# In-place product without a reset operand, carry kept as a running sum, first near factor on VectorE, in a chunked selective scan

## The chip, the cores and the metric

One Trainium2 chip, one of its cores. The metric is the device time of one execution in microseconds; the kernel before takes 9089.72 us, the median of 3 runs (9088.7 to 9092.31).

## The reference

Two layers on 4 images of 64x64 positions with 192 channels. Only the first layer's scan is touched. It runs over the 4096 positions in four directions k (rows, columns, and both reversed), with 384 channels d and 16 states n:

```python
delta = softplus(dts + delta_bias)
# one step per position, for every direction k, channel d, state n:
h = exp(delta * A[n]) * h + delta * B[n] * u
y = sum over n of h[n] * C[n]
```

`A[n]` is -n here, so the decay of state n over a stretch is the n-th power of one factor. The four y are added and normed over the channels, multiplied by a gate and projected.

## The kernel before, in words

The first layer (`FirstLayer`, L575) has three parts, `project`, `scans` (L759) and `finish`. The change lies in `scans` and in the constants that feed it.

**Rounds and states.** The sequence of each direction is cut into blocks of 30 positions. A *round* r is one block of all four directions and four images; there are NR = 137. A tile of a round has 128 rows and W = 1536 columns (4 images x 384 channels). Each half of 64 rows holds two directions: rows 0 to 59 are positions, and the last four (60 to 63) are for what is carried between blocks. A round goes through its 16 states one after the other, `state(s) = 16 - s % 16`, so that the loop at L1093 has 2192 *steps* s.

**Step s.** TensorE's `mix` (L1072) adds `b` times `x` into two accumulators `accs[0]` and `accs[1]` in PSUM, each 128 x 768. VectorE's `weigh` (L1081) then multiplies each in place by `fd`, the factor exp(SHIFT - sum of delta), so that a state's sum has been multiplied n times at the end (a Horner scheme over the powers). It is one `scalar_tensor_tensor` (L1088): accumulator times a column `hold_n`, times `fd`. At state 1 `end_y` (L959), a `tensor_tensor`, writes the product to SBUF instead.

**x.** `grown` (L1059) makes the next power of the input factor, six steps ahead (`AHEAD`): `x[s] = x[s-1] * f`. GpSimd does the 1024 *far* columns with `f` from SBUF, VectorE the 512 *near* columns with `f0` from PSUM (both L1070). The first power of a round is `dtu * g` (L1066); GpSimd does all of it, in three instructions of 512 columns, with near last. The `g` comes from ScalarE: `first_far` (L901, two parts) and `first_near` (L913).

**b.** `outer` (L1049, TensorE) and `cut_b` (L1057, VectorE), once per two steps, make the 64x64 weight blocks from B, C and the masks. Columns 60 to 63 of a block collect the sum over a block of positions, for even and odd states in different columns.

**Carry.** After every odd state ScalarE copies both accumulators (`keep_end`, L1025) before `weigh` changes them. DMAs cut the four last rows into `small` (`shrink`, L1013), GpSimd multiplies by the block's decay (`settle`, L1038), a DMA stores it in DRAM (`carry_out`, L1041), and one round later `carry_in` (L1020) brings two rows per half into rows 60 and 61 of `x`. `hold_n` is 0 in the carry rows at odd states and 1 elsewhere, so a carry row is emptied after each pair of states.

**Order.** The order on every engine, and that of SyncE's DMAs, is written out by hand (`manual_schedule`, L1091). A round's preparation is put at steps relative to its start (`steps`, L971). Those that matter: at -7 `sums_near` (TensorE, L910), at -6 `first_near` and `fall_near` (ScalarE, L913 and L917), at -6, -4 and -2 three extra `sums_d` on TensorE whose result nobody reads. Inside a step, VectorE does `weigh` for j = 0 and 1, then `grown`, then `cut_b` at even steps, then what is planned. All of the preparation uses one PSUM tile `m` of two banks at a time (`ps_p`, one buffer). In the following, a state pair is named by its steps within a round, 0 to 15; step -6 of the next round is step 10.

Of the kernel before, what the change touches and what calls it, by code (L numbers as in the profile page):

```python
# [10 lines left out]
F32 = mybir.dt.float32  # L11
AF = mybir.ActivationFunctionType
ALU = mybir.AluOpType

NB, HW, CH = 4, 64, 192
L = HW * HW
DI, NS, DR, KD = 384, 16, 12, 4
ND = DI // 128
CB, NC2 = 96, 2
LC = 512  # L20
# [9 lines left out]
RW = 30  # L30
PART = 4
NR = -(-L // RW)
HALF = 64
LP = NR * RW + 2
ND2 = 2 * DI
W = NB * DI
SHIFT = 2.5
# [534 lines left out]
            yield True  # L572


class FirstLayer(Stage):  # L575

    def __init__(self, tc, ctx, consts, w, dram, good):
        nc = tc.nc  # L580
        self.tc, self.w = tc, w
        self.ident, self.group, self.one = consts
        self.good = good
        self.uT, self.bc, self.xd, self.y_row, self.y_col, self.carry, self.zeros = dram
        wp = ctx.enter_context(tc.tile_pool(name="wf", bufs=1))

        def load(name, shape):
            t = wp.tile(shape, F32, name=f"{name}_f")
            nc.sync.dma_start(t, w[name])
            return t  # L590

        self.w_xd = load("w_xd", [128, ND, 64])
        self.w_bc = load("w_bc", [128, ND, KD * 2 * NS])
        self.w_dt = load("w_dtk", [128, DI])
        self.masks = load("masks", [128, 2, HALF])
        self.hold = load("hold", [128, 2])
        self.late = load("late", [128, NS // 2])
        self.gamma = load("gamma", [128, ND])
        self.beta = load("beta", [128, ND])
        self.ln_eps = wp.tile([128, 1], F32, name="ln_eps_f")  # L600
        nc.vector.memset(self.ln_eps, 1e-6)
        self.gn_eps = wp.tile([128, 1], F32, name="gn_eps_f")
        nc.vector.memset(self.gn_eps, GN_EPS)
        self.shift = {}
        for by in (1.0, -1.0, -NS):
            self.shift[by] = wp.tile([128, 1], F32, name=f"shift_{len(self.shift)}")
            nc.vector.memset(self.shift[by], by * SHIFT)
        self.minus = wp.tile([128, 128], F32, name="minus_f")
        nc.vector.tensor_scalar_mul(self.minus, self.ident, -1.0)
        self.far = wp.tile([128, 4 * W // 64], F32, name="far_f")  # L610
        a_col = load("a_col", [128, 1])
        nc.scalar.activation(a_col, a_col, AF.Exp)
        self.tri = load("steps", [128, 128])
        nc.vector.tensor_scalar_mul(self.tri, self.tri, a_col)
        self.dsum = wp.tile([128, DI], F32, name="dsum_f")
        with tc.tile_pool(name="d4", bufs=1) as pd:
            d4 = pd.tile([128, KD, DI], F32, name="d4")
            nc.sync.dma_start(d4, w["D_rows"].partition_broadcast(128))
            nc.vector.tensor_add(self.dsum, d4[:, 0, :], d4[:, 1, :])
            nc.vector.tensor_add(self.dsum, self.dsum, d4[:, 2, :])  # L620
            nc.vector.tensor_add(self.dsum, self.dsum, d4[:, 3, :])

            a_log = pd.tile([128, KD, ND, NS], F32, name="a_log")
            nc.sync.dma_start(a_log, w["A_log"])
            ref = pd.tile([128, KD], F32, name="a_ref")
            nc.sync.dma_start(ref, w["a_ref"].partition_broadcast(128))
            ln_n = pd.tile([128, NS], F32, name="ln_n")
            nc.sync.dma_start(ln_n, w["ln_n"].partition_broadcast(128))
            for k in range(KD):
                nc.vector.tensor_scalar(a_log[:, k], a_log[:, k], ref[:, k : k + 1], None, ALU.subtract)  # L630
            nc.vector.tensor_tensor(a_log, a_log, bc(bc(ln_n, 1, KD), 2, ND), ALU.subtract)
            nc.vector.tensor_mul(a_log, a_log, a_log)
            nc.vector.tensor_scalar(a_log, a_log, 1e-12, None, ALU.is_le)
            top = pd.tile([128, 1], F32, name="a_top")
            nc.vector.tensor_reduce(top, a_log.rearrange("p k d n -> p (k d n)"), mybir.AxisListType.X, ALU.min)
            nc.vector.tensor_tensor(self.good, self.good, top, ALU.min)

            z = pd.tile([128, W], F32, name="z")
            nc.vector.memset(z, 0.0)
            nc.sync.dma_start(self.zeros, z[:RW])  # L640
            near, end = NR // 2 * RW, LP - L
            for t in (*self.uT, self.y_row, self.y_col):
                nc.sync.dma_start(t[L:], z[:end].rearrange("p (b e) -> p b e", b=NB))
            for t in (self.xd, self.bc):
                nc.sync.dma_start(t[:, :, L:], z[: t.shape[0], : NB * end].rearrange("p (b l) -> p b l", b=NB))
            nc.sync.dma_start(self.y_col[near : near + RW], z[:RW].rearrange("p (b e) -> p b e", b=NB))
            for t in self.carry:
                nc.sync.dma_start(t, z[:, : 4 * W // 64])

    def run(self, srcs, dsts, gates):  # L650
        self.project(srcs, gates)
# [107 lines left out]
    def scans(self):  # L759
        nc, tc = self.tc.nc, self.tc  # L760
        with ExitStack() as ctx:
# [44 lines left out]
            class Round:  # L806
# [90 lines left out]

                def first_far(self, i):
                    if i == 1:
                        self.g = p1.tile([128, W], F32, name="g", tag="l")  # L900
                    nc.scalar.activation(self.g[:, wide(i)], self.m[:, 0, :], AF.Exp, bias=shift[-NS], scale=float(NS))  # L901

                def fall_far(self, i):
                    if i == 1:
# [5 lines left out]
                    nc.tensor.matmul(self.m[:, 0, :], tri, self.dt[:, wide(0)], start=True, stop=True)  # L910

                def first_near(self):
                    nc.scalar.activation(self.g[:, wide(0)], self.m[:, 0, :], AF.Exp, bias=shift[-NS], scale=float(NS))  # L913

                def fall_near(self):
                    self.f0 = ps_f.tile([128, LC], F32, name="f0")
# [74 lines left out]
                    r += [(at, "pe", s(self.sums_d, 0)) for at in (-6, -4, -2)]  # L991
                    return r

            w_dt, one, shift, zeros, hold, late = self.w_dt, self.one, self.shift, self.zeros, self.hold, self.late
            uT, bc_dram, xd_dram, y_row, y_col, carry = self.uT, self.bc, self.xd, self.y_row, self.y_col, self.carry
            MIDDLE = NR // 2
            AHEAD = 6
# [16 lines left out]

            def carry_in(s):
                n = state(s)
                v = carry[(n - 1) // 2].rearrange("(c p q r k) f -> p r q c (k f)", c=2, p=2, q=2, r=2)
                for r in range(2):
                    to = xs[s][r * HALF + 2 * RW : r * HALF + 2 * RW + 2].rearrange("q (c f) -> q c f", c=2)
                    nc.sync.dma_start(to, v[n % 2, r])  # L1020

            def keep_end(s, j):
                if j == 0:
# [14 lines left out]
                nc.gpsimd.tensor_tensor(back[s], back[s], small[s], ALU.mult)  # L1038

            def carry_out(s):  # L1040
                nc.sync.dma_start(carry[(state(s) - 1) // 2], back[s])  # L1041

            def outer(s):
                outs[s] = ps_o.tile([128, LC], F32, name="o")
# [14 lines left out]
            def grown(s, engine):  # L1059
                it = of(s)  # L1060
                if s not in xs:
                    xs[s] = p_x.tile([128, W], F32, name="x")
                if s % NS == 0:
                    if engine is nc.gpsimd:
                        for i in (1, 2, 0):
                            engine.tensor_tensor(xs[s][:, wide(i)], it.dtu[:, wide(i)], it.g[:, wide(i)], ALU.mult)  # L1066
                    return
                part = slice(0, LC) if engine is nc.vector else slice(LC, W)
                f = it.f0 if engine is nc.vector else it.f
                engine.tensor_tensor(xs[s][:, part], xs[s - 1][:, part], f, ALU.mult)  # L1070
# [10 lines left out]
            def weigh(s, j):  # L1081
                n = state(s)
                if n == 1:
                    of(s).end_y(j)
                    return
                hold_n = hold[:, n % 2 : n % 2 + 1]
                part = accs[j][:, :, :DI]
                nc.vector.scalar_tensor_tensor(part, part, hold_n, paired(of(s).fd, j), ALU.mult, ALU.mult)  # L1088

            engines = {e.engine for e in (nc.tensor, nc.scalar, nc.vector, nc.gpsimd, nc.sync)}  # L1090
            with tc.manual_schedule(engines=engines):  # L1091
# [577 lines left out]
def two_layer_vmamba(ctx: ExitStack, tc, x, out, ident, group, w0, w1):  # L1669
    nc = tc.nc  # L1670
# [17 lines left out]
    with ExitStack() as c0:  # L1688
# [3 lines left out]
            dr.tile([KD * DR, NB, LP], F32, name="xd"),  # L1692
            dr.tile([LP, NB, DI], F32, name="y_row"),
            dr.tile([LP, NB, DI], F32, name="y_col"),
            [dr.tile([128, 4 * W // 64], F32, name=f"carry{n}") for n in range(NS // 2)],
            dr.tile([RW, W], F32, name="zeros"),
        )
        layer = FirstLayer(tc, c0, (ident_t, group_t, one), w0, dram, good)
# [37 lines left out]
def _arrays(i):  # L1736
# [56 lines left out]
        steps[own, last] = steps[own, last + 2] = 1  # L1793
        which[own] = which[last] = k
    at_b = np.zeros((2 * NB, NS, 128), np.float32)
    masks, hold = np.zeros((128, 2, HALF), np.float32), np.ones((128, 2), np.float32)
    for k in range(KD):
        last = k // 2 * HALF + 2 * RW + k % 2
        own = slice(cols(k), cols(k) + RW)
        for p in range(2):  # L1800
            masks[own, p, k % 2 * RW : k % 2 * RW + RW] = steps[own, own]
            masks[last, p, k % 2 * RW : k % 2 * RW + RW] = 1
            masks[own, p, 2 * RW + 2 * p + k % 2] = masks[last, p, 2 * RW + 2 * p + k % 2] = 1
        hold[last] = hold[last + 2] = [1, 0]
        at_b[k // 2 * NB : (k // 2 + 1) * NB, :, last] = 1
    pairs = np.arange(NS // 2)
    late = [np.broadcast_to(-SHIFT * (2 * pairs + 2 - q), (32, NS // 2)) for q in range(2)]
    r["w0_w_dtk"], r["w0_grid"], r["w0_steps"] = wd, grid, steps
    r["w0_masks"], r["w0_hold"], r["w0_at_b"] = masks, hold, at_b
    r["w0_own"] = np.tile(np.eye(NB, dtype=np.float32), (2, 1))  # L1810
    r["w0_late"] = np.tile(np.concatenate(late), (2, 1)).astype(np.float32)
    a_log = f("A_logs").reshape(KD, DI, NS)
# [33 lines left out]
```

## Time and profile before

| what | us |
| --- | --- |
| median of 3 runs | 9089.72 |
| the profiled execution's own time | 9088.9 |
| its span | 9087.1 |
| `project` of the first layer | to about 700 |
| the loop of `scans`, first `weigh` to last | 707.7 to 7317.1 |
| the rest (first layer's `finish`, second layer) | 7317 to 9087 |
| one round | 48.3 |

The page's busy digits, in 40 slices of the span, with the granted clock of TensorE, the DMA share and its rate:

```profile
PE   8989999999999999999999999999999945887668
PEld 4433333333333333333333333333333335443457
DVE  3328999999999999999999999999999954796766
ACT  3336777777777777777777777777777745575668
POOL 0008999999999999999999999999999942001460
PEclk9999999999999999999999999999999977887789
DMA  6652222222222222222232233223223279343558
```

A digit is the busy share in tenths (9 is 90% or more). From slice 4 to slice 32, the loop, TensorE, VectorE and GpSimd all show 9; which of them sets the pace can't be seen from the digits. In the timeline a row is one instruction or several alike in a row (x2): start, duration, engine, line, output<-inputs, and in brackets the idle time of the engine before it with the instruction that ended it. `DVE` is VectorE, `ACT` ScalarE, `POOL` GpSimd, `PE` TensorE, `SPq` the DMA queue of SyncE.

### The profile page before, as it was taken

The numbers are of one execution on the slowest core, as the hardware profiler recorded it, in microseconds if no ns is written. First come the engines' busy times: TensorE is split into PE (matmuls) and PEld (weight loads), VectorE is DVE, ScalarE is ACT, GpSimd is POOL, SyncE is SP. The second block draws the span as 40 slices with busy tenths as digits, with TensorE's granted clock in tenths as the row PEclk, the third lists the DMA queues.
The fourth block names the chain that finished last, engine by engine and source line by source line (L and its number), as shares of the span: only waits on it lengthen the run. The fifth ranks groups of instructions, "written<-read, shape, count | busy, mean of one in ns | idle before, by whom it ended". The sixth has DMA issues, their size and how long they took to land. (4 is left out here: it accounts for less than half of the span.)

```text
span 9087.1 us, 193110 instructions
## 1 busy us (share of the span) xinstructions
PE 8310.9 (91%) x64280; PEld 3521.7 (39%) x64280; DVE 7681.2 (85%) x10101; ACT 6057.1 (67%) x10104; POOL 6790.2 (75%) x4088
## 2 busy tenths in 40 slices
PE   8989999999999999999999999999999945887668
PEld 4433333333333333333333333333333335443457
DVE  3328999999999999999999999999999954796766
ACT  3336777777777777777777777777777745575668
POOL 0008999999999999999999999999999942001460
PEclk9999999999999999999999999999999977887789
DMA  6652222222222222222232233223223279343558
GB/s 189 210 179 58 67 67 66 70 65 66 69 66 68 66 69 65 66 72 71 74 78 74 73 76 77 72 74 78 73 73 77 74 205 252 111 137 116 166 137 291
DMA packets 939211, 917.25 MB, mean 101 GB/s; under 512 B 554667, under 2 KB 807224, under 8 KB 937324
## 3 DMA queue, kind: packets, MB, share of 16 engines
q1 hardware_dynamic: 933148, 898.07, 36.2%
q0 software_dynamic: 5056, 6.66, 0.6%
q8 instruction: 521, 8.54, 0.4%
q14 instruction: 486, 3.98, 0.1%
HBM read 467.96 MB, written 375.75 MB: 93 GB/s over the span
## 5 line engine op out<-in xcount | busy, mean ns | idle before, releaser
L1070 POOL TENSOR_TENSOR x<-x,f 128x1024 f32<-128x1024 f32 x2055 | 4863.3, 2367 | 126.0 <-DMA carry<-back 27.1
L1088 DVE SCALAR_TENSOR_TENSOR acc<-acc,hold_f,fd 128x768 f32<-128x768 f32 x4110 | 4012.1, 1019 | 294.3 <-ACT sx L1025 266.4
L1076 PE MATMUL acc<-x,b 64*64 64x384 f32 x35072 | 3567.5, 502 | 95.4 <-DVE acc L937 78.8
L1025 ACT COPY sx<-acc 128x768 f32<-128x768 f32 x2192 | 1666.2, 808 | 736.5 <-PE acc L1076 707.7
L1076 PEld LDWEIGHTS acc<-x,b 64*64 64x64 f32 x35072 | 1004.3, 131 | 2245.4 <-DVE acc L1088 1842.0
L1070 DVE TENSOR_TENSOR x<-x,f 128x512 f32<-128x512 f32 x2055 | 1391.5, 677 | 18.8 <-ACT cs L834 15.6
L1049 PE MATMUL o<-cs,at_b 8*128 8x256 f32 x4384 | 1235.5, 400 | 2.0 <-DVE b L1057 2.0
L834 ACT ACTIVATE cs<-at_c,own 8x256 f32<-8x256 f32 x2192 | 1071.6, 495 | 5.9 <-PE o L1049 2.8
L1049 PEld LDWEIGHTS o<-cs,at_b 8*128 8x128 f32 x4384 | 726.9, 184 | 727.5 <-PE acc L1076 246.8
L1057 DVE TENSOR_TENSOR b<-o,masks_f 128x512 f32<-128x512 f32 x1096 | 749.1, 683 | 4.9 <-PE o L1049 4.9
L462 PE MATMUL pp<-xT,w_in 96*128 96x512 f32 x1536 | 713.7, 616 | 20.9 <-ACT pad L1284 20.3
L872 POOL TENSOR_SCALAR d<-l 128x1536 f32<-128x1536 f32 x137 | 201.4, 1470 | 665.3 <-ACT l L868 665.3
L1066 POOL TENSOR_TENSOR x<-dtu,g 128x512 f32<-128x512 f32 x411 | 517.1, 1272 | 138.1 <-ACT g L913 117.7
L842 PE MATMUL p<-dt,steps_f 64*64 64x384 f32 x5480 | 596.5, 505 | 7.4 <-ACT up L860 3.3
L901 ACT ACTIVATE g<-p,shift 128x512 f32<-128x512 f32 x274 | 188.3, 687 | 508.1 <-PE p L896 508.1
L859 ACT ACTIVATE e<-p 128x768 f32<-128x768 f32 x274 | 222.3, 811 | 435.9 <-PE p L842 419.1
L1298 DVE SCALAR_TENSOR_TENSOR acc<-pad,conv_w_s,acc 128x2048 f32<-128x2048 f32 x192 | 440.6, 2343 | 48.0 <-ACT acc L1296 46.7
L962 POOL TENSOR_TENSOR yt<-yt,yold 128x1536 f32<-128x1536 f32 x137 | 472.3, 3448 | 0.0
L1038 POOL TENSOR_TENSOR back<-back,small 128x96 f32<-128x96 f32 x1096 | 424.7, 388 | 15.0 <-DMA small<-sx 7.9
L462 PEld LDWEIGHTS pp<-xT,w_in 96*128 96x128 f32 x1536 | 292.0, 197 | 369.9 <-issue 341.1
L1035 ACT ACTIVATE back<-tot,late_f 128x96 f32<-128x96 f32 x1096 | 433.1, 395 | 0.0
L1279 POOL MEMSET pad<- 128x66 f32 x12 | 1.9, 159 | 556.2 <-DVE acc L1298 491.9
(217 smaller groups left out, 9496.0 us busy)
## 6 DMA issues: line engine op xcount, KB each, us to landing
ut<-uT SPq DMA_DIRECT2D x548, 180.0 KB
x<-carry SPq DMA_DIRECT2D x4384, 12.0 KB
small<-sx SPq DMA_DIRECT2D x2192, 24.0 KB
carry<-back SPq DMA_DIRECT2D x1096, 48.0 KB
zg<-gate SPq DMA_DIRECT2D x64, 768.0 KB
yold<-y_row SPq DMA_DIRECT2D x546, 90.0 KB
y_row<-yt SPq DMA_DIRECT2D x546, 90.0 KB
y_col<-yt SPq DMA_DIRECT2D x546, 90.0 KB
```

Of the source, the lines that this page charges most:

```text
L462: self.tc.nc.tensor.matmul(pp, self.w_in[:, i, e * 128 : (e + 1) * 128], self.xT[:, i, t * LC : (t + 1) * LC], start=(i == 0), stop=(i == ...
L834: nc.scalar.mul(self.cs[part][:, :, b, :], at_c[self.r % 2][:, at : at + PART, :], own[:, b : b + 1])
L842: nc.tensor.matmul(self.m[half(b), a, :DI], w(a, 2 * b + j), t(a, 2 * b + j), start=start and n == 0, stop=stop and n == len(terms) - 1, s ...
L962: nc.gpsimd.tensor_tensor(self.y, self.y, yold, ALU.add)
L1025: nc.scalar.copy(paired(sxs[s], j), accs[j][:, :, :DI])
L1049: nc.tensor.matmul(outs[s][:, at], at_b[p][:, n, :], cs[:, n % PART].rearrange("q b l -> q (b l)"), start=True, stop=True, skip_group_chec ...
L1057: nc.vector.tensor_tensor(bs[s], o, bc(masks, 2, NB), ALU.mult)
L1066: engine.tensor_tensor(xs[s][:, wide(i)], it.dtu[:, wide(i)], it.g[:, wide(i)], ALU.mult)
L1070: engine.tensor_tensor(xs[s][:, part], xs[s - 1][:, part], f, ALU.mult)
L1076: nc.tensor.matmul(accs[j][half(c), r, :DI], bs[s - s % 2][half(r), s % 2, b, :], xs[s][half(r), cols(b)], start=s % NS == 0, stop=state(s ...
L1088: nc.vector.scalar_tensor_tensor(part, part, hold_n, paired(of(s).fd, j), ALU.mult, ALU.mult)
L1298: nc.vector.scalar_tensor_tensor(acc, part(tap), weight(tap), acc, ALU.mult, ALU.add)
```

## The change

- `hold` is gone. `weigh` is a plain `tensor_tensor` in place, `acc * fd`. The carry rows are no longer emptied, and go on through the states as the other rows do.
- So a pair's carry holds also what the pair above it left (the state two up). Next round this is taken away: `carry_in` brings four rows per half rather than two, the pair's own and those of the pair above, into rows 60 to 63 of `x`; `at_b` has the factor -exp(2 SHIFT) for the upper pair's row, and `masks` lets it through.
- For that, the eight carry tensors in DRAM become one, with pair as an inner axis and a ninth pair of zeros. `carry_out` writes four pieces instead of one contiguous block.
- `first_near` writes to the second bank of the PSUM tile `m` (`m[:, 1]`) instead of to `g` in SBUF, and VectorE does the near 512 columns of the first power in its ordinary place (`grown` at step -6). GpSimd does the other 1024 in one instruction.

The core of the diff:

```diff
+def carry_of(t, m):
+    return t[:, :, m].rearrange("c p q r f -> (c p) (q r f)")
...
-            for t in self.carry:
-                nc.sync.dma_start(t, z[:, : 4 * W // 64])
+            for m in range(NS // 2 + 1):
+                nc.sync.dma_start(carry_of(self.carry, m), z[:, : 4 * W // 64])
...
-                        self.g = p1.tile([128, W], F32, name="g", tag="l")
-                    nc.scalar.activation(self.g[:, wide(i)], self.m[:, 0, :], AF.Exp, bias=shift[-NS], scale=float(NS))
+                        self.g = p1.tile([128, W - LC], F32, name="g", tag="l")
+                    nc.scalar.activation(self.g[:, wide(i - 1)], self.m[:, 0, :], AF.Exp, bias=shift[-NS], scale=float(NS))
...
                 def first_near(self):
-                    nc.scalar.activation(self.g[:, wide(0)], self.m[:, 0, :], AF.Exp, bias=shift[-NS], scale=float(NS))
+                    nc.scalar.activation(self.m[:, 1, :], self.m[:, 0, :], AF.Exp, bias=shift[-NS], scale=float(NS))
...
             def carry_in(s):
                 n = state(s)
-                v = carry[(n - 1) // 2].rearrange("(c p q r k) f -> p r q c (k f)", c=2, p=2, q=2, r=2)
+                m = (n - 1) // 2
+                v = carry[:, n % 2, m : m + 2].rearrange("c m q r f -> r (m q) c f")
                 for r in range(2):
-                    to = xs[s][r * HALF + 2 * RW : r * HALF + 2 * RW + 2].rearrange("q (c f) -> q c f", c=2)
-                    nc.sync.dma_start(to, v[n % 2, r])
+                    to = xs[s][r * HALF + 2 * RW : (r + 1) * HALF].rearrange("q (c f) -> q c f", c=2)
+                    nc.sync.dma_start(to, v[r])
...
-                nc.sync.dma_start(carry[(state(s) - 1) // 2], back[s])
+                nc.sync.dma_start(carry_of(carry, (state(s) - 1) // 2), back[s])
...
                 if s % NS == 0:
-                    if engine is nc.gpsimd:
-                        for i in (1, 2, 0):
-                            engine.tensor_tensor(xs[s][:, wide(i)], it.dtu[:, wide(i)], it.g[:, wide(i)], ALU.mult)
+                    part, g = (slice(0, LC), it.m[:, 1, :]) if engine is nc.vector else (slice(LC, W), it.g)
+                    engine.tensor_tensor(xs[s][:, part], it.dtu[:, part], g, ALU.mult)
                     return
...
-                hold_n = hold[:, n % 2 : n % 2 + 1]
-                part = accs[j][:, :, :DI]
-                nc.vector.scalar_tensor_tensor(part, part, hold_n, paired(of(s).fd, j), ALU.mult, ALU.mult)
+                acc = accs[j][:, :, :DI]
+                nc.vector.tensor_tensor(acc, acc, paired(of(s).fd, j), ALU.mult)
...
-            [dr.tile([128, 4 * W // 64], F32, name=f"carry{n}") for n in range(NS // 2)],
+            dr.tile([2, 2, NS // 2 + 1, 2, 2, ND2], F32, name="carry"),
...
-        hold[last] = hold[last + 2] = [1, 0]
+            masks[last + 2, p] = masks[last, p]
         at_b[k // 2 * NB : (k // 2 + 1) * NB, :, last] = 1
+        at_b[k // 2 * NB : (k // 2 + 1) * NB, :, last + 2] = -math.exp(2 * SHIFT)
```

More of the change, by code (lines that the diff above doesn't have):

```diff
@@ L595, in __init__ @@
         self.masks = load("masks", [128, 2, HALF])
-        self.hold = load("hold", [128, 2])
         self.late = load("late", [128, NS // 2])
@@ L992, in steps @@
                     return r
-            w_dt, one, shift, zeros, hold, late = self.w_dt, self.one, self.shift, self.zeros, self.hold, self.late
+            w_dt, one, shift, zeros, late = self.w_dt, self.one, self.shift, self.zeros, self.late
             uT, bc_dram, xd_dram, y_row, y_col, carry = self.uT, self.bc, self.xd, self.y_row, self.y_col, self.carry
@@ L1795, in _arrays @@
     at_b = np.zeros((2 * NB, NS, 128), np.float32)
-    masks, hold = np.zeros((128, 2, HALF), np.float32), np.ones((128, 2), np.float32)
+    masks = np.zeros((128, 2, HALF), np.float32)
     for k in range(KD):
@@ L1808, in _arrays @@
     r["w0_w_dtk"], r["w0_grid"], r["w0_steps"] = wd, grid, steps
-    r["w0_masks"], r["w0_hold"], r["w0_at_b"] = masks, hold, at_b
+    r["w0_masks"], r["w0_at_b"] = masks, at_b
     r["w0_own"] = np.tile(np.eye(NB, dtype=np.float32), (2, 1))
```

## The prediction

> **What bounds the kernel now.** I read the page's busy rows first, then the groups by shape, VectorE's timeline over a round, and last ScalarE's and TensorE's timelines around the places where VectorE is idle. On the page:
>
> ```profile
> PE 8310.9 (91%) x64280; PEld 3521.7 (39%) x64280; DVE 7681.2 (85%) x10101; ACT 6057.1 (67%) x10104; POOL 6790.2 (75%) x4088
> ...
> L1070 POOL TENSOR_TENSOR x<-x,f 128x1024 f32<-128x1024 f32 x2055 | 4863.3, 2367 | 126.0 <-DMA carry<-back 27.1
> L1088 DVE SCALAR_TENSOR_TENSOR acc<-acc,hold_f,fd 128x768 f32<-128x768 f32 x4110 | 4012.1, 1019 | 294.3 <-ACT sx L1025 266.4
> ```
>
> The loop of the scans takes 6609 of the 9087 us, and all rounds last 48.3 us. In one round (window 2999.46 to 3047.73) VectorE is busy 45.77 us, GpSimd 46.54, TensorE 47.16 by modelled ends. VectorE's idle time of 2.5 us is nearly all before L1088, ended by ScalarE's copy `sx`. The timeline of VectorE shows both kinds of step pair, first a waiting one, then a full one:
>
> ```profile
> 3005.42 1.95 DVE L1088 SCALAR_TENSOR_TENSOR acc<-acc,hold_f,fd 128x768 f32<-128x768 f32 x2 [0.38 <-ACT sx L1025]
> 3007.28 0.68 DVE L1070 TENSOR_TENSOR x<-x,f 128x512 f32<-128x512 f32 x1
> 3007.87 1.94 DVE L1088 SCALAR_TENSOR_TENSOR acc<-acc,hold_f,fd 128x768 f32<-128x768 f32 x2
> 3009.73 0.68 DVE L1057 TENSOR_TENSOR b<-o,masks_f 128x512 f32<-128x512 f32 x1
> ...
> 3029.09 1.94 DVE L1088 SCALAR_TENSOR_TENSOR acc<-acc,hold_f,fd 128x768 f32<-128x768 f32 x2
> 3030.95 0.68 DVE L1070 TENSOR_TENSOR x<-x,f 128x512 f32<-128x512 f32 x1
> 3031.54 1.94 DVE L1088 SCALAR_TENSOR_TENSOR acc<-acc,hold_f,fd 128x768 f32<-128x768 f32 x2
> 3033.39 0.68 DVE L1070 TENSOR_TENSOR x<-x,f 128x512 f32<-128x512 f32 x1
> 3033.99 0.68 DVE L1057 TENSOR_TENSOR b<-o,masks_f 128x512 f32<-128x512 f32 x1
> 3034.59 1.94 DVE L1088 SCALAR_TENSOR_TENSOR acc<-acc,hold_f,fd 128x768 f32<-128x768 f32 x2
> ```
>
> From start to start two L1088 take 1.86 us, so 0.93 each, and a 512-column product 0.59 to 0.60. From 3029.09 to 3034.59 VectorE never waits: 4 x 0.93 + 2 x 0.59 + 0.60 = 5.50. The pair that starts at 3005.42 lasts 5.97, to 3011.39, and its second step has no x product (L1070 is absent: it is the first power, step 10, which GpSimd does) but ends in 0.99 us idle. What it waits for:
>
> ```profile
> 3009.39 0.69 ACT L913 ACTIVATE g<-p,shift 128x512 f32<-128x512 f32 x1 [1.48 <-PE p L910]
> 3009.98 0.65 ACT L917 ACTIVATE f<-p,shift 128x512 f32<-128x512 f32 x1
> 3010.55 0.81 ACT L1025 COPY sx<-acc 128x768 f32<-128x768 f32 x1
> ```
>
> The copy stands behind two exponentials, these behind `sums_near` on TensorE (3008.23, 1.12 us), this behind `mix` of the step before, and that behind the second L1088 of the pair's *first* step. So this pair's length is a ring: two in-place products, mix, sums, two exponentials, copy. VectorE is a member of the ring, but with two of its four products only.
>
> **The product (L1088).** Nothing in the trace is this product without `hold`, in place in PSUM. The nearest rows:
>
> ```profile
> L887 DVE TENSOR_TENSOR dtu<-p,ut 128x768 f32<-128x768 f32 x124 | 117.8, 950 | 0.0
> L959 DVE TENSOR_TENSOR yt<-acc,fd 128x768 f32<-128x768 f32 x124 | 112.9, 953 | 25.1 <-ACT sx L1025 25.1
> ...
> L937 DVE TENSOR_TENSOR acc<-acc,tot 128x96 f32<-128x96 f32 x62 | 16.0, 258 | 0.0
> ```
>
> L959 has the same operands, but writes to SBUF: 953 ns against 1019, and 0.87 us from start to start (two take 1.74, 3023.37 to 3025.11) against 0.93. L937 works in place in PSUM: 258 ns for 96 columns; the L887 and L1070 rows give (950-677)/256 = 1.07 ns a column, so its fixed part is 155 ns, against 950-820 = 130 for L887. In place thus costs at most 25 ns more; the bounds are 950 and 978 ns, and as L937 follows its successor after only 0.17 us I take 958. Saved: 0.06 us each, 30 in a round, 1.8 us of VectorE's time (bounds 1.2 and 2.0).
>
> A rule of the Trainium skill speaks against this saving. "VectorE: DVE Perf Modes", section "The TRN2 errata", puts a VectorE instruction's cost at 120 cycles plus a cycle an element at 0.96 GHz when it reads PSUM, whatever the operation: 925 ns for 768 columns, with or without `hold`. By the rule the saving is 0 and the change worth nothing or, if the new product below lies open, 0.66 x 137 = 90 us of loss. The rows (1019 and 953, same inputs, both reading PSUM) show that the operation matters, and I go by the rows.
>
> **How much reaches the end.** By pairs of steps, odd step to odd step, mean over 100 rounds from the starts of L1088 (before, and with the change):
> - 1 to 3, never waiting: 5.49, all four products count, -0.24. Its copy ended about 0.2 us before it was needed; that cover is just used up.
> - 3 to 5 and 5 to 7: 6.51 and 6.62, closed by rings over one step's products, x, `dtu` (L887), TensorE, copy (idle 0.08 and 0.18): -0.12 each. VectorE's own work would fall by 0.24, so the idle grows.
> - 7 to 9, 9 to 11, 11 to 13, 13 to 15: 5.96 to 6.02, the ring above, or the same with `v` and `parts` in place of sums and exponentials: -0.12 each. TensorE alone could follow down to 0.17 less (its second mix was free to start at 3007.25 and began at 3007.42), so it doesn't end later.
> - 15 to 1: 5.72; `end_y` is already a plain product, and the first product of step 0 is hidden behind the second `mix`, which waits for L937: -0.06.
>
> Sum: 0.24 + 6 x 0.12 + 0.06 = 1.02 us a round.
>
> **The first near product.** VectorE gets one product of 512 columns with PSUM input per round, as L1057: 683 ns, 0.60 from start to start (bounds 0.59 and 0.68). Its place is step 10, behind the two L1088 and ahead of L1057, where the 0.99 us of idle time are. It adds a wait on `first_near`: queued behind it are L1057 and the next `weigh`. By the old clock, shifted by the 0.12 of the ring: products done 3009.49, `first_near` ends 3009.96 (writing PSUM it may be 27 ns faster, as L917 653 against L906 680), product to 3010.6, L1057 to 3011.2, and the copy lets `weigh` go at 3011.27. It fits by some 0.07 us: cost 0, up to 0.1 if the handover is slower; 0.6 (82 us in all) if there were no hole. The tile `m` is released by VectorE some 0.17 us later than by L917, so the unread `sums_d` (3010.69) and `outer` behind it slip; `mix` then starts 0.1 late, but VectorE is behind its x product then, 0.3 later: 0 (bound 0.05).
>
> **GpSimd.** Three L1066 (1.27 each, and 0.86 idle for L913) become one product of 1024 columns as L1070, 2.37: -1.44 busy, -0.86 wait a round. GpSimd runs more than one step ahead, so this pays nothing itself. It is a cover, however: 46.54 of 48.27 us busy would stand against a round of 47.3; with the change it is 45.1.
>
> **Carry.** 32 `x<-carry` DMAs a round go from 12 to 24 KB: 0.38 MB in 47 us, 8 GB/s on top of 66 to 72, with DMA share 0.29. SyncE's issues fill 37.8 of 48.3 us (the carry-ins 0.247 each). Bounds: 0 to 0.08 each (L828's issue lasts 0.32), and the store in four pieces 0 to 0.15 (`small<-sx` 0.57 against 0.42): below 3.8 us a round in a queue with 10 us of waiting in it. A carry is stored 6 steps before it is read and lands 3 steps before its `mix`: 0. The lost `hold` load and the ninth zero DMA: 0.
>
> **The sum.** 1.0 us x 137 rounds = 137 us: 9088.9 - 137 = 8952 for the profiled execution; the median of the runs lies 0.8 higher, so 8953.
>
> **Rivals.**
> - *All of VectorE's saving counts* (the copies move up because TensorE is ahead more than I see): 1.8 x 137 = 250, so 8840. Against it: six of eight pairs are rings. 7%.
> - *The hole is too small*: the wait on `first_near` and later `outer` cost 0.3 to 0.6, or the product is nearer 978: a gain of 0.4 to 0.7, 8994 to 9035. For it: the fit is 0.07 us. 17%.
> - *No change*: rule right, product hidden; or 0.6 of gain against 0.6 of open product. 5%.
> - *Slower: the one carry tensor.* Eight separate tensors become one with interleaved pieces. If the program then orders each carry-in behind the store issued just ahead of it (in the same step, on the same queue), SyncE stands still until the store lands, 8 times a round. The only landing times in the trace are those of GpSimd's stores, 2.8 to 3.9 us; with 2.8, 37.8 + 22.4 = 60.2 us a round, SyncE is the bound: +1600 us, 10700. It decides from (48.3 - 37.8)/8 = 1.3 us a store on. Against it: the slots read and the slot written are different addresses. 11%; with other mishaps the slower side has 14%.
>
> **Numbers.** Forecast 8953, 57%. The range reaches over the second rival and a bit to the first: 8910 to 9045. Faster by over 0.2% 0.81, within 0.2% (about what a measurement here can tell from no change) 0.05, slower 0.14.
>
> **What would show it.** L1088 a TENSOR_TENSOR of about 958 ns; in the round, VectorE's idle before it 3.0 us or so, still ended by `sx`; a 512-column product at step 10 that waits some 0.4 us for L913, with the idle time after it nearly gone; no L1066 of 512 columns on GpSimd; rounds of 47.3 us. I am wrong if the in-place product stays above 1 us, if GpSimd or a carry DMA ends VectorE's waits, or if SyncE waits for `carry<-back` ahead of L1020.

## The result: slower by 1.65%, and the profile after

The changed kernel takes 9237.11 us (median of 4 runs, 9235.5 to 9238.84) against 9089.21 (4 runs, 9079.06 to 9092.31): ratio 1.0165, 95% interval 1.0147 to 1.0182. The forecast was 8953, range 8910 to 9045. The profiled execution has a span of 9236.7 us. The page of the changed kernel, busy rows and the groups that answer to those of before:

```profile
PE 8325.8 (90%) x64280; PEld 3607.3 (39%) x64280; DVE 7548.9 (82%) x10238; ACT 6071.9 (66%) x10104; POOL 6605.4 (72%) x3814
...
L1073 POOL TENSOR_TENSOR x<-x,f 128x1024 f32<-128x1024 f32 x2055 | 4864.3, 2367 | 578.4 <-DMA small<-sx 103.6
L1090 DVE TENSOR_TENSOR acc<-acc,fd 128x768 f32<-128x768 f32 x4110 | 3776.2, 959 | 391.5 <-ACT sx L1029 309.9
```

Read for themselves, these lines say that the change worked. The product takes 959 ns, not 1019; VectorE is busy 132 us less and GpSimd 185 less. But GpSimd's group now waits 578 us, so something else sets the pace. The loop of `scans`, first `weigh` to last, in the view by windows (columns: stretch, its length, busy time of PE, PEld, DVE, ACT and POOL with instructions, granted TensorE clock, DMA share, GB/s). Before:

```profile
707.70:7317.00 6609.30, 6447.62 (x56560) 2367.40 (x56553) 6263.03 (x7935) 4695.04 (x8046) 6354.68 (x3827) 1.00 0.29 71
```

and after:

```profile
710.84:7466.90 6756.06, 6472.91 (x56560) 2459.12 (x56552) 6131.09 (x8071) 4710.63 (x8047) 6170.49 (x3555) 0.97 0.31 77
```

The loop is 146.8 us longer. It begins 3.1 us later, and what follows it takes as long as before (1769.8 and 1770.1 us). The clock has gone from 1.00 to 0.97. The lengths of the rounds, from the starts of `weigh`, fall into three groups: 70 *quiet* ones of 48.27 us, as long as before's, 33 of 51.1 and 25 of 49.9; a few lie outside these. All rounds together exceed 48.27 each by 152 us, before's by 5. Two questions follow: where the forecast 1.02 us a round went in the quiet rounds, and what makes the others long.

**The quiet rounds.** VectorE's timeline at step 10 of a round, after the change:

```profile
1036.01 1.83 DVE L1090 TENSOR_TENSOR acc<-acc,fd 128x768 f32<-128x768 f32 x2 [0.50 <-ACT sx L1029]
1037.75 0.68 DVE L1073 TENSOR_TENSOR x<-x,f 128x512 f32<-128x512 f32 x1
1038.35 1.82 DVE L1090 TENSOR_TENSOR acc<-acc,fd 128x768 f32<-128x768 f32 x2
1041.32 0.69 DVE L1069 TENSOR_TENSOR x<-dtu,p 128x512 f32<-128x512 f32 x1 [1.15 <-issue]
1041.92 0.68 DVE L1061 TENSOR_TENSOR b<-o,masks_f 128x512 f32<-128x512 f32 x1
1042.52 0.96 DVE L1090 TENSOR_TENSOR acc<-acc,fd 128x768 f32<-128x768 f32 x1
```

and ScalarE's beside it:

```profile
1039.87 0.66 ACT L916 ACTIVATE p<-p,shift 128x512 f32<-128x512 f32 x1 [1.37 <-PE p L913]
1040.57 0.66 ACT L920 ACTIVATE f<-p,shift 128x512 f32<-128x512 f32 x1
1041.15 1.50 ACT L1029 COPY sx<-acc 128x768 f32<-128x768 f32 x2
```

The pair lasts 6.51 us (1036.01 to 1042.52); the forecast was 5.97 - 0.12 = 5.85. The new product (L1069) waits 1.15 us, to 1041.32. Its operand, the output of `first_near` (L916), was done at 1040.53. What ends just before 1041.32 is `fall_near` (L920), at 1041.23, 89 ns earlier, and ScalarE's last instruction to end before this product is `fall_near` in all 137 rounds. The view names no releaser ("issue"), but the trace has the wait itself: VectorE's sequencer waits ahead of L1069 for ScalarE's semaphore, until 1041.27, 44 ns after `fall_near`. Both `first_near` and `fall_near` touch the PSUM tile `m`, from which the product now reads. `fall_near` also starts 34 ns after `first_near` has ended, where before it started 0.10 us ahead of that (3009.98 against 3010.08), and in the trace it now waits for ScalarE's own semaphore, which it didn't before. It reads bank 0 of `m` alone and `first_near` writes bank 1 alone: the program orders the two banks as if they were one.

**The long rounds.** TensorE's timeline at this place before, where no idle time stands between `mix` and the unread `sums_d` (L842):

```profile
3009.29 1.52 PE L1076 MATMUL acc<-x,b 64*64 64x384 f32 x16
3010.69 0.88 PE L842 MATMUL p<-dt,steps_f 64*64 64x384 f32 x8
```

and after the change:

```profile
1039.76 1.52 PE L1079 MATMUL acc<-x,b 64*64 64x384 f32 x16
1042.06 0.88 PE L845 MATMUL p<-dt,steps_f 64*64 64x384 f32 x8 [0.78 <-DVE x L1069]
1042.87 1.12 PE L1053 MATMUL o<-cs,at_b 8*128 8x256 f32 x4
```

and the windows from 1040 us:

```profile
1040.00:1042.00 2.00, 1.28 (x16) 0.30 (x8) 0.85 (x3) 1.97 (x4) 1.92 (x2) 1.00 0.54 147
1042.00:1044.00 2.00, 1.94 (x16) 0.95 (x20) 2.00 (x4) 1.30 (x3) 2.00 (x3) 1.00 0.40 119
1044.00:1046.00 2.00, 2.00 (x16) 0.55 (x16) 1.90 (x3) 0.51 (x1) 1.33 (x1) 0.64 0.22 43
1046.00:1048.00 2.00, 2.00 (x16) 0.61 (x16) 1.76 (x3) 0.25 (x1) 1.66 (x1) 0.50 0.24 59
```

The unread `sums_d` (L845) that fills TensorE's time here writes to `m` as well, so it waits for L1069, and TensorE is idle 0.78 us. Two to three microseconds later the granted clock is 0.50. In that state 16 matmuls of `mix` take 2.27 to 2.84 us, not 1.52, and the steps behind wait for TensorE. In the loop the clock stands at 0.50 in 62 stretches, 337.9 us in all; before, in one of 3.4 us. The rounds' whole excess lies there: the 63 rounds with time at half clock exceed 48.27 by 153 us together, the 73 others by nothing (-0.8).

### The profile page after: what moved, and what is told of

It is laid out like the page before. It is cut to its first block, busy times and chain, and to the rows that moved or that the text cites. A ratio compares the mean times of both kernels' runs of the same rounds, so it can differ in the third digit from the quotient of the medians.

```text
span 9236.7 us, 194062 instructions
## 1 busy us (share of the span) xinstructions
PE 8325.8 (90%) x64280; PEld 3607.3 (39%) x64280; DVE 7548.9 (82%) x10238; ACT 6071.9 (66%) x10104; POOL 6605.4 (72%) x3814
## 5 line engine op out<-in xcount | busy, mean ns | idle before, releaser
L1090 DVE TENSOR_TENSOR acc<-acc,fd 128x768 f32<-128x768 f32 x4110 | 3776.2, 959 | 391.5 <-ACT sx L1029 309.9
L1079 PE MATMUL acc<-x,b 64*64 64x384 f32 x35072 | 3515.9, 511 | 85.7 <-DVE acc L940 78.2
L1079 PEld LDWEIGHTS acc<-x,b 64*64 64x64 f32 x35072 | 1080.6, 134 | 2073.4 <-DVE acc L1090 1493.3
L845 PE MATMUL p<-dt,steps_f 64*64 64x384 f32 x5480 | 620.9, 525 | 155.6 <-DVE x L1069 107.9
L549 PE MATMUL op<-w_out,v 128*128 128x192 f32 x1536 | 288.1, 345 | 139.7 <-DVE ot L552 101.2
```

The lines of the kernel that those rows point to most:

```text
L845: nc.tensor.matmul(self.m[half(b), a, :DI], w(a, 2 * b + j), t(a, 2 * b + j), start=start and n == 0, stop=stop and n == len(terms) - 1, s ...
L1079: nc.tensor.matmul(accs[j][half(c), r, :DI], bs[s - s % 2][half(r), s % 2, b, :], xs[s][half(r), cols(b)], start=s % NS == 0, stop=state(s ...
L1090: nc.vector.tensor_tensor(acc, acc, paired(of(s).fd, j), ALU.mult)
```

## The experiments

The theory (A in the expectations) was: the product's gain is real; the first near product, placed on VectorE, waits for `fall_near` and holds back `cut_b`, the unread `sums_d`, `outer` and `mix`; this both eats the gain and lets TensorE's clock fall. Its rivals: the new carry DMAs, through SyncE, cost what was lost (B); the in-place product frees less than it should (C); the clock falls for a reason that has nothing to do with TensorE's idle time. Diffs are against the kernel named.

**product_only**, before with the plain product alone:

```diff
-                hold_n = hold[:, n % 2 : n % 2 + 1]
-                nc.vector.scalar_tensor_tensor(part, part, hold_n, paired(of(s).fd, j), ALU.mult, ALU.mult)
+                nc.vector.tensor_tensor(part, part, paired(of(s).fd, j), ALU.mult)
```

> The kernel before with the plain in-place product (L1088 without hold) and nothing else; it leaves out the emptying of the carry rows, so the carried sums are too large and the time alone is read. Theory A (the loss comes from the first near product: it waits for fall_near as well as first_near because both read the shared PSUM tile m, and the hole this makes on TensorE lets its clock be halved): the product's own share is as forecast, rounds of 47.3 us, about 8950, no stretch at half clock. Theory B (the loss comes from the carry: 24 KB carry-ins, one tensor, SyncE): the same, about 8950. Theory C (a faster product gains nothing, because the rings over ScalarE and TensorE set every pair): 9075 to 9090.

Measured: 8967.4 us, ratio 0.9868 (0.9851 to 0.9884), quiet rounds 47.44 us, clock as before. The product is worth 122 us when it is alone. By pairs of steps, from odd step to odd step, differences of the medians over the rounds:

| pair | forecast, ns | measured, ns |
| --- | --- | --- |
| 15 to 1 | -60 | -9 |
| 1 to 3 | -240 | -209 |
| 3 to 5 | -120 | -124 |
| 5 to 7 | -120 | -1 |
| 7 to 9 | -120 | -123 |
| 9 to 11 | -120 | -123 |
| 11 to 13 | -120 | -120 |
| 13 to 15 | -120 | -118 |

Five pairs are within 10 ns. The largest miss is 5 to 7: VectorE's idle time there grows from 175 to 415 ns, by all of the 240 that four products save. TensorE works in that pair without a gap from `mix` of step 5 to the sums (L896), which start 3.47 us after `weigh` before and after the change. So no in-place product is in that ring, nor is `dtu` (L887), which is now done 0.19 us before the sums start. 15 to 1 misses 51 ns and 1 to 3 misses 31; these weren't followed up.

**near_only**, before with the first near product alone moved to VectorE:

```diff
... (`g` narrowed to the far columns)
-                    nc.scalar.activation(self.g[:, wide(0)], self.m[:, 0, :], AF.Exp, ...)
+                    nc.scalar.activation(self.m[:, 1, :], self.m[:, 0, :], AF.Exp, ...)
...
-                    if engine is nc.gpsimd:
-                        for i in (1, 2, 0):
-                            engine.tensor_tensor(xs[s][:, wide(i)], it.dtu[:, wide(i)], it.g[:, wide(i)], ALU.mult)
+                    part, g = (slice(0, LC), it.m[:, 1, :]) if engine is nc.vector else (slice(LC, W), it.g)
+                    engine.tensor_tensor(xs[s][:, part], it.dtu[:, part], g, ALU.mult)
```

> The kernel before with the first near product moved to VectorE, its factor in the second bank of m; hold and carry as before. Theory A: as slow as the changed kernel or slower, 9200 to 9300: the product starts 0.09 us after fall_near ends, step 10's pair grows by about 0.65 us, and part of the rounds show TensorE at half clock for 3.4 or 6.8 us. Theory B: as before, 9080 to 9095. Theory C: 9090 to 9170 (the 0.6 us of the added product lie open, 82 us).

Measured: 9261.18 us, 1.0199 (1.0182 to 1.0216): 172 us of loss by this part alone. Quiet rounds are 48.95 us, +0.69, and 35 half-clock stretches of 177 us in all have appeared. No carry DMA is changed in this kernel, so the carry isn't needed for the loss.

**first_on_gpsimd**, the changed kernel with the first power back on GpSimd (the reverse of the diff above):

> The changed kernel with the first power given back to GpSimd as a whole, its near factor in SBUF, as in the kernel before; plain product and new carry stay. Theory A: 8950 to 8970, rounds of 47.3 us and the clock at 1.00 through the loop; GpSimd is then busy 46.5 of 47.3 us and may add some tenths of a us. Theory B: about as slow as the changed kernel, 9200 or more. Theory C: 9075 to 9095.

Measured: 9011.3 us, 0.9922 (0.9906 to 0.9939), quiet rounds 47.45. That is above the 8950 to 8970 of theory A; what is missing is the carry's, as the runs from tot_early on show. So the rest of the change is a gain of 78 us, and the moved product costs 226 on top of it. With product_only this divides the loop's time: product -113.5 us, carry +33.2 (6529.0 against 6495.8), first near product +227.1. The sum is +146.8 because each is a difference to the kernel one step on; it isn't a test. The parts don't simply add up: in near_only the moved product costs the loop 166 us, not 227, with 35 half-clock stretches, not 62. And the carry's 33 us, nearly all in the second half of the loop, don't show in the changed kernel, whose halves are alike (3359.9 and 3357.2 us for 68 rounds each): they are paid when the rounds are short.

**order**, the changed kernel, at step 10 with `cut_b` ahead of the first near product on VectorE, and `outer` ahead of the unread `sums_d` on TensorE:

```diff
-                    if on(s + AHEAD):
+                    late_x = (s + AHEAD) % NS == 0
+                    if on(s + AHEAD) and not late_x:
                         grown(s + AHEAD, nc.vector)
                     if on(s + 2) and s % 2 == 0:
                         cut_b(s + 2)
+                    if on(s + AHEAD) and late_x:
+                        grown(s + AHEAD, nc.vector)
...
-                    planned(s, "pe")
+                    if not late_x:
+                        planned(s, "pe")
                     if on(s + 4) and s % 2 == 0:
                         outer(s + 4)
+                    if late_x:
+                        planned(s, "pe")
```

> The changed kernel with two neighbours swapped in step 10 alone: VectorE does cut_b ahead of the first near product, TensorE does outer ahead of the unread sums_d. The waits stay, but cut_b and outer no longer stand behind them. Theory A: TensorE's hole is filled by outer, no half clock, the near product is hidden behind the copy of the next pair: 8950 to 8985. Theory B: 9200 or more, as the carry is unchanged. Theory C: 9090 to 9110.

Measured: 9019.53 us, 0.9927 (0.9911 to 0.9944), quiet rounds 47.56, 6 half-clock stretches. VectorE's timeline at step 10 of this kernel:

```profile
839.63 0.68 DVE L1061 TENSOR_TENSOR b<-o,masks_f 128x512 f32<-128x512 f32 x1
840.87 0.69 DVE L1069 TENSOR_TENSOR x<-dtu,p 128x512 f32<-128x512 f32 x1 [0.55 <-issue]
```

`cut_b` now fills 0.6 us of the hole and TensorE has `outer` to do. The product still waits for `fall_near`. The order of two instructions on each of two engines is worth 218 us. The move to VectorE as such was not the fault; what stood behind its wait was.

**before_no_fill**, before without the three unread `sums_d`, to see whether TensorE's idle time is what lets the clock fall:

```diff
-                    r += [(at, "pe", s(self.sums_d, 0)) for at in (-6, -4, -2)]
```

> The kernel before without the three unread sums_d of a round (at steps -6, -4 and -2), nothing else; the result doesn't change. Theory A (a hole on TensorE lets its clock be halved for whole stretches of 3.4 us): stretches at half clock in part of the rounds, the granted clock of the loop below 1.00, 9110 to 9300. Rival (the half clock in the changed kernel has another cause, such as power or the denser VectorE): clock 1.00 as before, 9070 to 9092, as TensorE has less to do.

Measured: 9351.35 us, 1.0291 (1.0272 to 1.031). It does less work, changes nothing else, and its loop is 290 us longer (6899.4 us). The loop in the view by windows:

```profile
698.00:7600.00 6902.00, 6564.66 (x53300) 2419.52 (x53292) 6296.56 (x7938) 4696.58 (x8053) 6359.99 (x3831) 0.93 0.27 68
```

3260 matmuls fewer, and PE is busy 117 us *longer*, since the clock is 0.50 for 948.9 us in 92 stretches. The 28 rounds without half clock are as long as before's. So the matmuls that nobody reads are what kept the clock full in before. That the late one in the changed kernel does its damage by the same way is what order and fall_late bear on: the one has `outer` in the hole, the other moves the filler away from it, and both keep the clock.

**fall_late**, the changed kernel with `fall_near` one step later, behind the copies, and the unread `sums_d` behind it:

```diff
-(-6, "act", self.first_near), (-6, "act", self.fall_near)]
+(-6, "act", self.first_near), (-5, "act", self.fall_near)]
...
-for at in (-6, -4, -2)]
+for at in (-5, -4, -2)]
```

> The changed kernel with fall_near one step later (-5 instead of -6), behind that step's copies on ScalarE, and the unread sums_d of -6 moved to -5. Theory A (the first near product waits for fall_near, which reads the other bank of the same PSUM tile): the product starts right behind first_near, some 0.65 us earlier, step 10 loses its extra length, quiet rounds are 47.3 to 47.5 us; with the clock held 8975 to 9025, and if the hole left by the moved sums_d lets the clock drop in some rounds, up to 9080. Rival (it waits for something else, a DMA or GpSimd): the product starts 1.15 us after weigh as before, 9200 or more.

Measured: 9090.97 us, 1.0005 (0.9995 to 1.0014), no change against before, 146 better than the changed kernel, but outside the expected 8975 to 9080. VectorE, and TensorE behind it:

```profile
840.56 0.69 DVE L1069 TENSOR_TENSOR x<-dtu,p 128x512 f32<-128x512 f32 x1 [0.45 <-POOL x L1069]
...
843.02 1.52 PE L1079 MATMUL acc<-x,b 64*64 64x384 f32 x16
844.36 0.82 PE L845 MATMUL p<-dt,steps_f 64*64 64x384 f32 x8
845.27 0.87 PE L845 MATMUL p<-w_dtk_f,xd 26*64 26x384 f32 x8
```

L1069 waits 0.45 us instead of 1.15 and starts 88 ns behind the end of `first_near` (the view puts the wait down to GpSimd's L1069, which had ended 0.41 us before): that the old wait was for `fall_near` is shown. But the round stays at 48.2 us. The unread `sums_d` (844.36), one step later, stands ahead of `v` (845.27) on TensorE, which closes the next ring: step 12 takes 0.83 us more (4365 ns). A filler has its price where TensorE is in the ring. The clock held (4 half-clock stretches), although TensorE's hole at step 10 is as long as in the changed kernel (0.78 us): so idle time of that length is not enough by itself.

The remaining cost of 33 us for the carry was looked at next. Before, SyncE's own timeline shows (L1020 carry-in, L1041 store)

```profile
1001.42 0.53 SPq L1020 DMA_DIRECT2D x<-carry  x2
...
1003.87 0.42 SPq L1041 DMA_DIRECT2D carry<-back  x1
```

and in first_on_gpsimd

```profile
1002.85 0.73 SPq L1024 DMA_DIRECT2D x<-carry  x2
...
1005.03 0.56 SPq L1045 DMA_DIRECT2D carry<-back  x1
```

Over the loop the issue of a carry-in takes 0.34 us in the changed kernel against 0.25, that of a store 0.58 against 0.41: 32 x 0.094 + 8 x 0.17 = 4.4 us more a round; the mean sum of SyncE's issues is 34.5 us a round before and 39.0 after. Most of the harm is in the loop's second half, where `load_y` has 8 transfers a round, not 4 (3227.3 us in the first, 3262.8 in the second). Waits of ScalarE from 4400 to 7200 us (columns: us in total, times, longest) in product_only:

```profile
ACT tot L934 <- DMA tot<-fd: 0.6, 1, 0.6
```

and in first_on_gpsimd:

```profile
ACT tot L937 <- DMA tot<-fd: 71.2, 59, 2.6
```

**tot_early**, first_on_gpsimd with that DMA (`keep_total`) issued two steps earlier:

```diff
-                    r += [(-4, "sp", self.keep_total),
+                    r += [(-6, "sp", self.keep_total),
```

> The changed kernel with the first power back on GpSimd, as in first_on_gpsimd, and keep_total's two DMAs issued two steps earlier in SyncE's order (-6 instead of -4), so that they don't stand behind as many carry DMAs. Theory D (what first_on_gpsimd lacks against product_only, 44 us, is SyncE running late in the second half of the loop, where log_total on ScalarE then waits for tot<-fd): 8970 to 8990. Rival E (it is the doubled carry traffic or its landing, wherever it waits): 9000 to 9015.

Measured: 9012.18 us, 0.9916 (0.99 to 0.993), no gain over first_on_gpsimd. The wait for `tot<-fd` fell from 95 to 4 us over the whole loop, and `mix` at step 0 now waits for its carry-in in the second half instead. That this one DMA was at fault is refuted; whether SyncE as a whole is late, or the doubled traffic counts, this run doesn't tell.

**two_rows**, first_on_gpsimd with carry-ins of two rows as before, from the new carry tensor:

```diff
-                v = carry[:, n % 2, m : m + 2].rearrange("c m q r f -> r (m q) c f")
+                v = carry[:, n % 2, m].rearrange("c q r f -> r q c f")
...
-                    to = xs[s][r * HALF + 2 * RW : (r + 1) * HALF].rearrange(...)
+                    to = xs[s][r * HALF + 2 * RW : r * HALF + 2 * RW + 2].rearrange(...)
```

> first_on_gpsimd with carry-ins of two rows per half again (only the pair's own sum, 12 KB each); it leaves out the subtraction of the pair above, so the carried sums are too large and the time alone is read. The store in four pieces and the one tensor stay. Theory D (what first_on_gpsimd lacks against product_only is SyncE running late by the longer issues of the carry-ins, 0.344 instead of 0.247 us each): 8968 to 8980, second half of the loop as fast as the first. Rival F (it is the store, 0.58 instead of 0.41 us, or the one tensor's ordering): 9000 to 9015.

Measured: 8976.36 us, 0.9882 (0.9865 to 0.9898), loop 6498.0 us, its halves 3226.4 and 3232.5. 31 of the carry's 33 us are gone. The carry's cost comes from the carry-ins of four rows, not from the single tensor and not from the store. They take longer to issue and move twice the bytes; no run parts the two.

**gpsimd_spread**, tot_early with `load_y` five steps later, where SyncE has less to do; **order_tot**, order with `keep_total` two steps earlier; and **order_spread**, order_tot with `load_y` later too:

```diff
-                    r += [(10, "sp", self.load_y),
+                    r += [(15, "sp", self.load_y),
```

> tot_early with load_y's DMAs moved from step 10 to step 15 of SyncE's order, where no other planned load stands; they are needed at step 5 of the next round. Theory D: SyncE catches up between its crowded steps, carry-ins no longer arrive late for mix in the second half: 8970 to 8995. Rival E (traffic, not order): 9005 to 9015.

> The changed kernel with the swaps of order and keep_total two steps earlier. Theory D: 8980 to 9000, as order's second half of the loop is slowed by the same wait. Rival E: 9012 to 9025.

> order_tot with load_y's DMAs moved from step 10 to step 15. Theory D: 8982 to 8998 (quiet rounds stay 47.56 us). Rival E: 9010 to 9020.

Measured: gpsimd_spread 9001.23 us, 0.9904 (0.9888 to 0.9921), second half 3250.8 us. order_tot 9015.91, 0.9921 (0.9908 to 0.9934), second half 3246.3 against order's 3266.5. order_spread 9010.31, 0.9913 (0.9896 to 0.9929), second half 3258.2: GpSimd's `add_old` now waits 87 us for the load that was moved. Each takes a part of the loss in the second half and opens another; between these three the intervals overlap, so their order isn't settled. Of the runs that moved DMAs, tot_early, order_tot and order_spread fall into the range of rival E (the doubled traffic) and gpsimd_spread between E's and D's, so that SyncE's order is the cause is not shown.

**fall_late2**, the changed kernel with what the runs had taught: `fall_near` at -5, no unread `sums_d` at -6 (those at -4 and -2 stay), `keep_total` at -6, `load_y` at 15:

> The changed kernel with fall_near at step -5 behind the copies, as in fall_late, but without the unread sums_d there (fall_late's stood ahead of v on TensorE and lengthened the ring of steps 11 to 13 by 0.83 us), and with keep_total and load_y moved as in order_spread. Theory A with the clock held: quiet rounds 47.4 us, 8970 to 8990. If the missing sums_d lets the clock drop in part of the rounds: 9050 to 9150 with stretches at half clock after step 10.

Measured: 8997.6 us, 0.99 (0.9883 to 0.9916), quiet rounds 47.42, clock held. VectorE at step 10:

```profile
838.81 0.69 DVE L1069 TENSOR_TENSOR x<-dtu,p 128x512 f32<-128x512 f32 x1 [0.45 <-POOL x L1069]
```

(Here too the view names GpSimd's L1069, which ended 0.40 us earlier; `first_near` ended at 838.73.) The first near product stays on VectorE and costs nothing in a quiet round (47.42 against 47.45 with it on GpSimd), and the kernel beats both before and after. TensorE still has a hole of 0.77 us at step 10, with `outer` and a whole `mix` behind it and no `sums_d`, and the clock falls in 3 stretches only.

## Why the prediction was wrong, step by step

- **The product.** Right: 958 ns forecast, 959 measured. The rule of the Trainium skill that spoke against it ("VectorE: DVE Perf Modes", "The TRN2 errata") gave 925 ns with or without `hold`; its row is for results that go to SBUF and names no operation. Measured are 1019 ns with it and 959 without: the figure fits neither, and the operation matters, as the prediction held.
- **How much reaches the end.** Nearly right: 1.02 us a round forecast, 0.83 measured in product_only. The missed terms are pair 5 to 7 (-0.12 forecast, 0.00 measured), which was called a ring over one step's products, but they aren't in it; 15 to 1 (-0.06, -0.01); and 1 to 3 (-0.24, -0.21). 137 x 0.83 = 114 us, the loop's gain.
- **The first near product: "It fits by some 0.07 us: cost 0."** This is the step that failed. It added one wait, on `first_near`, and set the start at that one's end. Measured, the product starts at the end of `fall_near`, 0.7 us later. The prediction had seen that `m` is shared and put the cost on the wrong side: it had `m` released later *by* VectorE, and never asked who else was in `m` ahead of it. The pair took 6.51 us, not 5.85, and the steps 11 to 13 another 0.16: together the 0.82 us between the quiet rounds of 48.27 and 47.45. That the wait is on `fall_near` is shown by the trace's wait and by fall_late. That it comes from the sharing of one tile is argued, from the two instructions' operands and from `fall_near`'s new wait for `first_near`; no run with two tiles was made.
- **The "unread `sums_d`" that slip, "0 (bound 0.05)".** This is the second half of the failure, and the larger. TensorE was idle 0.78 us, and what follows that hole is light work; the granted clock fell, which the prediction didn't consider: 153 us, more than the whole net loss. The 0.82 us of the quiet rounds come to 112. The prediction even names these matmuls as unread and doesn't ask what they are for.
- **The hole too small** (8994 to 9035, 17%). The hole was too small, but for the wait on `fall_near`, which this rival didn't name, and at a higher price: 0.82 us a round in the quiet rounds against "0.3 to 0.6". Quiet rounds are as long as before's, so without the fall of the clock the kernel would have come out at about no change.
- **Carry: "0".** The bounds were a little too low (0.08 and 0.15 us an issue; 0.094 and 0.17 measured), and the waiting in the queue was no full cover in the second half, which has more transfers. (The 37.8 us a round include some 4 us in which SyncE waits; the issues of that round are 33.7.) Cost: 33 us in rounds of 47.4 us, near the length that was forecast, and nothing that shows in the longer rounds of the changed kernel. **The carry-ordering rival** (10700) did not come: no carry-in stood still behind a store for its landing.
- **GpSimd.** Right: three products became one, and busy time fell by 185 us against 1.44 x 137 = 197.

What would have shown it: "the 0.99 us idle hole" was followed by a list of what the new wait depends on; the list needed every reader and writer of the tile, and every instruction queued behind, on TensorE too.

## What to carry to other kernels

An instruction put into a hole waits for all that touches its operands' buffer, not only for its producer; so list all readers and writers of the tile, and put what doesn't need the wait (`cut_b`, `outer`) ahead of it. Matmuls whose result nobody reads can be there to hold the clock; before a change delays one, cost the stage at half the clock. When a sum of parts comes out wrong, run each part alone: here -122 for the product, +172 for the moved one and +44 for the carry told where to look. They sum to +94 and not to the +148 that was measured, for the parts act on each other: the rounds at half clock lose 77 us in near_only and 153 in the changed kernel.

## What the runs showed of the hardware

- **The clock falls without an idle window.** In the loop of the changed kernel all 62 drops to 0.50 start on one grid of 3413 ns and last 3.41, 6.83 or 10.24 us. "TensorE: Matmul & The Clock Gate" of the Trainium skill gives a window of this length (Part 1) and lets the clock fall after a whole idle one; its section "A second HAM failure mode" says that short idle times between groups of matmuls can do it too. Here one drop follows an idle window (TensorE stood still for 5.10 us in the middle of the loop). The other 61 follow none, and 60 of these drops have the hole of step 10 in the window before them.
- **What sorts the windows is the work in them, not the idle time.** Take for each window of the grid at full clock the sum over its matmuls of rows times streamed columns (64 x 384 = 24,576 for one of `mix`, 8 x 256 = 2,048 for one of `outer`), a matmul on an edge by its share. In the loops of all 14 traces these are 26,533 windows, and 215 are followed by a drop. All 215 have at most 380,340; of the other 26,318 only 5 have as little, all within 1% of that. Half of before's windows have more than 660,000, and its lowest that was spared has 400,000. Busy time sorts worse: of windows busy for less than 0.78 of their length, 62 of 107 drop in the changed kernel, but 4 of 117 in fall_late and 3 of 108 in fall_late2, whose lowest spared windows have 400,000 and 391,000. So the hole by itself does little. It hurts where it lies in one window with the unread `sums_d` and `outer` (8 rows), so that little of a `mix` fits in: in 60 of the 62 cases it begins in the first sixth of the window. The figure was fitted after the fact to these kernels' shapes, with modelled ends of matmuls; it is no rule for others. A round of 48.27 us is 14.14 windows, so the hole wanders over the grid, which fits with some rounds being hit and others not.
- **An issue grows with its pieces, not its bytes alone.** The same 48 KB stored as one block take SyncE 0.41 us, in four pieces 0.58. A carry-in of 12 KB in 4 pieces takes 0.25 us, of 24 KB in 8 pieces 0.34; there both grow.
